# A graph attention layer under a list schedule: allowances on dependences between engines, later small products, and no weight plane on GpSimd

## The chip, the cores and the metric

The kernel runs on one core of a Trainium2 chip. The core has five engines with one instruction queue each: TensorE (PE, with its weight loads as PEld), VectorE (DVE), ScalarE (ACT), GpSimd (POOL) and SyncE (SP, which here only issues DMAs). They run side by side and wait for each other by semaphores. The metric is the time of the launch in microseconds (us); lower is better.

## The reference

One layer of a graph network on 384 nodes with 1024 features. LayerNorm and relu, three projections, a second projection of each, attention of 16 heads of 64 with an additive mask that is built from 6528 edges, an output projection and the residual:

```
h = relu(layernorm(x))                       # 384 x 1024
q, k, v = h @ wq.T + bq, h @ wk.T + bk, h @ wv.T + bv
q2, k2, v2 = (q @ wiq.T + biq), (k @ wik.T + bik), (v @ wiv.T + biv)   # 16 heads of 64
mask = full((384, 384), -inf)
mask[src, dst] = softplus(edge_type_weights)[edge_type - 1]   # the last write of a cell holds
scores = q2 @ k2.T / 8 + mask                # each head
out = softmax(scores) @ v2
return x + out @ wo.T + bo
```

(On the diagonal, a cell that no edge has set gets the fourth weight.) Everything is float32.

## The kernel before, in words

**Products.** Each float32 operand is split in two planes, hi and lo, and a product is three matmuls in a row, hi·hi, hi·lo and lo·hi (`mm3`, L448, L449, L450). The seven 1024 x 1024 weights are read as 56 chunks of 512 KB: v is chunks 0 to 7, q 8 to 15, iv 16 to 23, k 24 to 31, then iq and ik in turns 32 to 47, and o 48 to 55. For each chunk SP loads it (`raw`, or `scan` for a first pass that only sums up norms, L146), ACT makes the hi plane (`split_hi`, L121 or L125) and `split_lo` the lo plane: L132 with a scale, L134 without. L134 runs on DVE, but a list of flags, `lop`, puts it on POOL for chunks 10 and 30 (its flag for 21 has no effect, since only v, q and k chunks are asked). Chunk 1's lo plane is POOL's too, written out in the head.

**Small products.** Scales are taken from bounds, which PE sums over partitions with products of eight or nine columns (L530, L535), or turns around with a transpose. Task names: bv (bound of v), biv, turn (maximum of q), kb, v2t, gq, gk and ob. bv needs the eight v tiles: each is scaled by DVE (`v_f`, L477) and biased and summed by ACT (`v_e`, L480 and L481).

**Mask.** DVE detects for each of 51 columns of 128 edges which of them a later edge overwrites (L293), and forms indices (L299, L300). POOL scatters each column with an indirect DMA into one of three tables in DRAM (L304). When all are done POOL loads the tables (L312, three times `mbs`, 128 x 1152), DVE merges each (L316, three times `ma`), and scales the three row blocks (L567).

**Attention.** For each pair of heads p (0 to 7) and block of 128 rows there is a step S(j), j = 3p to 3p + 2: six matmuls (L702) into the two PSUM banks of tag `s`. DVE adds the mask and reduces (L710, twice), which frees the banks for S(j + 1); ACT takes the exponential (L714), DVE the reciprocal (L717, L721), POOL normalises some of the tiles (L724), ACT makes hi planes (L729, L731) and POOL or DVE the lo planes (L735, L737). SP turns them with DMA transposes (L742), and PE multiplies by v2 (L751, "av"). ACT and DVE split the result (L755, L758), and the o product reads it. DVE finishes seven pieces (L772) with residual x + bo, which POOL has added up before (`residual`, L778, six times), and SP writes them out.

**What sets the order.** After the head, every operation is a task: an engine, an estimated duration, dependences and a lag. PE's order comes from numbers in the table P: chunks follow each other, the small products have a place of their own (`sp`), S(j) is placed at TB + pre + j · rate + ds[j] (TB is the end of chunk 31), av and o relative to it. A loop then picks, again and again, the ready task with the smallest pair (start, due) over all engines, where due is worked back from those who need it, and emits it. So P decides what stands before what in each engine's queue; the queues run in order. The start of a task is the end of what it depends on, plus the lag where that is on another engine; PE's tasks have another allowance, `slack`, on top. `sdl` says how long a scatter takes to land.

Of the kernel before, what the change touches and what calls it, by code (L numbers as in the profile page):

```python
# [23 lines left out]


P = dict(
    pre=11.3,
    rate=2.57,
    avlag=7,
    slack=0.42,  # L30
    act0=6.95,
    dve0=4.68,
    pool0=7.97,
    pb=6,
    lead=3,
    gate=2.88,
    sdl=4.44,
    mll=3.72,
    ds=[0.0, 0.0, 0.0, 0.0, 0.0, 0.0, 0.0, 0.0, 0.0, 0.0, 0.0, 0.62, 0.0, 1.11, 0.0, 0.0, 0.0, 0.0, 0.0, 0.0, 0.0,
        0.0, 0.0, 0.67],  # L40
    da=[1.19, 1.19, 1.19, 1.19, 1.19, 0.13, 0.13, 0.13],
    pool=[0, 1, 0, 1, 0, 1, 0, 1, 0, 1, 0, 1, 0, 1, 0, 1, 0, 1, 0, 1, 0, 1, 0, 1, 0, 0, 0, 1, 0, 1, 0, 1, 0, 1, 0,
        1, 0, 1, 0, 1, 0, 1, 0, 1, 0, 1, 0, 1],
    lop=[0, 0, 0, 0, 0, 0, 0, 0, 0, 0, 1, 0, 0, 0, 0, 0, 0, 0, 0, 0, 0, 1, 0, 0, 0, 0, 0, 0, 0, 0, 1, 0],
    last=[3, 1, 2, 0, 4, 6, 5],
    sp=dict(row=5.6, bv=37.0, biv=53.34, turn=69.41, kb=88.0, v2t=110.0, gq=118.19, gk=128.67, ob=150.0),
    due=dict(v2l=-0.13, ss=-0.34, gkd=-2.65),
)


# [1 line left out]
def gnn_kernel(ctx: ExitStack, tc: tile.TileContext, x, edges, erows, etw, wq, wk, wv, wiq, wik, wiv, wo,  # L52
# [74 lines left out]
    def split_lo(w, eng=None):  # L127
        if w < NCH:
            hi, lo = whl[w]
            sc = weight_scale(w)  # L130
            if sc is not None:
                nc.vector.scalar_tensor_tensor(lo, raw[w], sc, hi, op0=OP.mult, op1=OP.subtract)  # L132
            else:
                (eng or nc.vector).tensor_tensor(lo, raw[w], hi.bitcast(F32), OP.subtract)  # L134
# [520 lines left out]
    bob = scan[:, 2, :]  # L655
# [10 lines left out]
    def task(name, eng, dur, fn, deps=(), lag=0.2, takes="", frees_at=None):  # L666


        tasks[name] = (eng, dur, fn, [d for d in deps if d in tasks or d in end], lag)
        alloc[name] = takes.split()  # L670
        frees[name] = frees_at or []
# [6 lines left out]
    def chunk_mm(c, k):  # L678
        if k == 0:
            gps[c] = bank("g")  # L680
        colmm(gps[c], c, {"iq": qT, "ik": kT.get("t")}.get(chunks[c][0], hT), k)
# [112 lines left out]
    def planes_tasks(c):  # L794
        n = chunks[c][0]
        if c >= 5:
            task(("load", c), "SP", 1.46, lambda: load(c), [("lo", c - 4), ("load", c - 1)], 0.95)
        if c >= 3:
            task(("hi", c), "ACT", 0.95 if n in "vqk" else 1.04, lambda: split_hi(c),
                 [("load", c), ("hi", c - 1), {"iv": "bivd", "iq": "gqd", "ik": "gkd", "o": "obd"}.get(n, "")], 0.2,  # L800
                 "w w" if n in "vqk" else "w", [final(c)] if n != "o" else ["never"])
        if c >= 2:
            pool = c < 32 and n in "vqk" and P["lop"][c]
            task(("lo", c), "POOL" if pool else "DVE", 2.3 if pool else 1.2,
                 lambda: split_lo(c, POOL if pool else None), [("hi", c)])

    def chunk0():
        gps[0] = ps = bank("g")
# [10 lines left out]
    def chunk_tasks(c):  # L819
        n, m = chunks[c]  # L820
        planes_tasks(c)
        before = final(c - 1) if c else ""
        if c == 0:
            task(("mm", 0, 7), "PE", 4.2, chunk0, [("lo", 0)], 0.2, "g", [evict(0)])
        elif n == "iv":
            for i in range(6):
                task(("mm", c, i), "PE", 0.65, lambda i=i: iv_mm(m, i),
                     [("lo", c), ("vlo", m), before] if i == 0 else [("mm", c, i - 1)], 0.2,
                     "ssroag"[i] if m == 0 else "", [("v2l", i) if i < 5 else "early"])
        else:  # L830
            for k in range(KT):
                task(("mm", c, k), "PE", 0.52 if c < 32 else 0.49, lambda k=k: chunk_mm(c, k),
                     [("lo", c), before] if k == 0 else [("mm", c, k - 1)], 0.2, "" if k else "g", [evict(c)])

    def pe_sums(name, bankname, fn, deps, users):
# [126 lines left out]
        task(("aohi", p), "ACT", 0.56, lambda p=p: ao_hi(p), [("av", p), "home"])  # L962
        task(("aolo", p), "DVE", 0.53, lambda p=p: ao_lo(p), [("aohi", p)])
    for i in range(6):
        task(("res", i), "POOL", 1.2, lambda i=i: residual(i), [("xb", i // 2), "bob"])
    OFROM = [[], ["ob"], [("mm", 47, 0)], [("mm", 47, 0), ("o", 2, 0)], [("S", J - 1)], [("S", J - 1), ("o", 4, 0)],
             [("mm", 47, 0), ("o", 3, 0)]]
    for k in range(8):
# [58 lines left out]
    def needed(n):  # L1027
        if n not in due:
            eng, dur, _, _, lag = tasks[n]
            due[n] = 0.0  # L1030
            far = n[0] == "sc"
            d = min([needed(u) - (P["sdl"] + 1 if far and u != ("sc", n[1] + 1) else 0 if tasks[u][0] == eng else lag)
                     for u in users[n]], default=now) - dur
            k = "elo" if n[0] == "lo" and len(n) == 3 else n[0] if isinstance(n, tuple) else n
            due[n] = min(d, at.get(n, d)) + P["due"].get(k, 0.0)
        return due[n]
# [10 lines left out]
    while left:  # L1047
        best = None
        for n, (eng, dur, _, deps, lag) in left.items():
            if not all(d in end for d in deps):  # L1050
                continue
            start = max([free[eng], free["port"] if port(n, eng) else 0.0])
            for d in deps:
                e = tasks.get(d, ("", 0, 0, 0, 0.0))
                start = max(start, end[d] + (0 if e[0] == eng else e[4] + (P["slack"] if eng == "PE" else 0)))
            if eng == "SP" and 0 < dur and n[0] != "turn":
                start = max(start, free["DMA"] - P["gate"])
            ok = True
            for i, tag in enumerate(alloc[n]):
                w = len(ring[tag]) + alloc[n][:i].count(tag) - RING[tag]  # L1060
                for f in ring[tag][w] if w >= 0 else []:
                    if f in end:
                        start = max(start, end[f] + (0 if tasks[f][0] == eng else tasks[f][4]))
                    else:
                        ok = False
            if ok:
                rank = (start, at[n] if eng == "PE" else needed(n))
                if best is None or rank < best[0]:
                    best = rank, n
        if best is None:  # L1070
            raise ValueError(str([(n, [d for d in left[n][3] if d not in end], alloc[n]) for n in list(left)[:12]]))
        (start, _), n = best
        eng, dur, fn, _, lag = left.pop(n)
        end[n] = free[eng] = start + dur
        if port(n, eng):
            free["port"] = end[n]
        if eng == "SP" and 0 < dur and n[0] != "turn":

            free["SP"] = start + 0.48
            end[n] = free["DMA"] = max(free["DMA"], start + 1.1) + dur  # L1080
        if n[0] == "sc":
            end["sd", n[1]] = max(free["DMA"], start + 1.0) + P["sdl"]
        for i, tag in enumerate(alloc[n]):
            ring[tag].append([frees[n][i]] if len(frees[n]) > i else [])
        fn()
# [39 lines left out]
```

## Time and profile before

| | |
|---|---|
| three runs | 280.84, 280.05, 282.71 us; median 280.84 |
| the profiled execution | 280.18 us, of which 278.5 are its span |
| mean granted PE clock | 0.994 |
| busy PE, DVE, ACT, POOL | 267.0, 213.3, 207.1, 141.5 us |
| matmuls | 1629 |

The span runs from the first to the last instruction that the profiler sees; 1.7 us of the time lie outside it. A row of a timeline gives the start in us from the span's start, the duration in us, the engine, the line of the program, the operation, output <- inputs by the program's names, shapes, and in brackets the engine's idle time before it with what ended that. PE's matmuls overlap: the step from one start to the next counts, not the duration. A window's row gives each engine's busy time in a stretch and the granted clock of PE, 1.00 at full speed.

### The profile page before, as it was taken

Reading aid. Unit: us, or ns where it says so; the run is one execution under the profiler, and the core shown is the slowest. Engines: PE = TensorE matmul, PEld = TensorE weight load, DVE = VectorE, ACT = ScalarE, POOL = GpSimd, SP = SyncE. Lnnn points to the kernel's source line nnn. Section 1 sums busy time; section 2 is a strip of 40 time slices with the busy share of each in tenths; the row PEclk is TensorE's granted clock in tenths of the full one; section 3 lists DMA queues with packets and bytes.
Section 4 is the critical chain, followed back from the end, with each engine's and each line's share of the span. In section 5 each row is a group of like instructions: output and inputs, shape, how many; then the busy total and the mean of one; then the engine's idle time right before and its main releaser. Section 6 shows DMA issues by size and latency. Waiting matters only on the chain.

```text
span 278.5 us, 4982 instructions
## 1 busy us (share of the span) xinstructions
PE 267.0 (96%) x1629; PEld 186.7 (67%) x1629; DVE 213.3 (77%) x531; ACT 207.1 (74%) x394; POOL 141.5 (51%) x150
## 2 busy tenths in 40 slices
PE   7999999699999999999999969999999999999995
PEld 5899999599984444899996534545555554444542
DVE  4876679999999634577869597888889997996334
ACT  3898699698989964669859447799889989747300
POOL 4768857465565645105744087556664365505200
PEclk9999999999999999999999997999999999999999
DMA  7799997899999977578688972798989999983706
GB/s 255 258 320 410 402 404 290 335 407 328 345 384 409 401 260 280 175 270 317 236 283 319 373 286 75 125 204 184 210 192 160 225 199 189 243 203 81 141 2 226
DMA packets 59546, 72.44 MB, mean 260 GB/s; under 512 B 42624, under 2 KB 44160, under 8 KB 59520
## 3 DMA queue, kind: packets, MB, share of 16 engines
q1 hardware_dynamic: 57456, 70.32, 80.8%
q0 software_dynamic: 2064, 1.80, 2.2%
q8 instruction: 13, 0.21, 0.3%
q14 instruction: 13, 0.11, 0.1%
HBM read 59.27 MB, written 3.39 MB: 225 GB/s over the span
## 4 chain that ended last, share of the span: by engine, by line
PE 59%; DMA 13%; DVE 11%; ACT 8%; issue 5%; POOL 3%; SPq 1%; DVEq 0%; POOLq 0%; ACTq 0%
PE g L448 13%; PE g L449 13%; PE g L450 13%; DMA scan<-in_wiv_dram 4%; PE s L702 4%; DMA raw<-in_wik_dram 3%; PE a L751 3%; PE s L448 2%; PE s L450 2%; PE s L449 2%; DMA pt<-pp 2%; DMA raw<-in_wo_dram 2%; DVE e L710 2%; DMA g<-in_x_dram 2%; DVE whl L132 2%
## 5 line engine op out<-in xcount | busy, mean ns | idle before, releaser
L448 PE MATMUL g<-g,whl 128*128 128x384 f32 (+1 forms) x312 | 104.7, 336 | 0.0
L449 PE MATMUL g<-g,whl 128*128 128x384 f32 (+1 forms) x312 | 103.8, 333 | 0.0
L450 PE MATMUL g<-g,whl 128*128 128x384 f32 (+1 forms) x312 | 103.8, 333 | 0.0
L304 POOL DMA_INDIRECT tab<-edge x51 | 57.6, 1129 | 39.1 <-DMA tab<-edge 24.1
L146 ACT ACTIVATE scan<-scan 128x1024 f32<-128x1024 f32 x40 | 41.9, 1049 | 8.5 <-DMA scan<-in_wik_dram 4.9
L735 POOL TENSOR_TENSOR pp<-e,pp 128x384 f16<-128x384 f32 x23 | 23.5, 1021 | 29.1 <-ACT pp L729 28.9
L448 PEld LDWEIGHTS g<-g,whl 128*128 128x128 f32 x184 | 34.6, 188 | 2.9 <-DVE whl L134 2.8
L450 PEld LDWEIGHTS g<-g,whl 128*128 128x128 f32 x184 | 34.5, 188 | 0.1
L449 PEld LDWEIGHTS g<-g,whl 128*128 128x128 f32 x184 | 34.6, 188 | 0.0
L714 ACT ACTIVATE e<-e,st 128x384 f32<-128x384 f32 x48 | 29.0, 605 | 7.3 <-DVE st L710 6.7
L134 DVE TENSOR_TENSOR whl<-raw,whl 128x1024 fp32r<-128x1024 f32 x20 | 24.8, 1243 | 11.9 <-ACT whl L125 11.7
L710 DVE CUSTOM_DVE_ANT_0 e<-s,ma,cols 128x384 f32<-128x384 f32 x48 | 27.9, 612 | 4.6 <-PE s L702 3.3
L724 POOL TENSOR_TENSOR e<-e,st 128x384 f32<-128x384 f32 x23 | 23.3, 1015 | 15.9 <-DVE st L721 15.5
L125 ACT ACTIVATE whl<-raw 128x1024 fp32r<-128x1024 f32 x23 | 24.2, 1052 | 2.8 <-DMA raw<-in_wv_dram 2.0
L121 ACT ACTIVATE whl<-raw,cols 128x1024 f16<-128x1024 f32 x16 | 18.0, 1138 | 7.1 <-DMA raw<-in_wiq_dram 3.3
L132 DVE SCALAR_TENSOR_TENSOR whl<-raw,cols,whl 128x1024 f16<-128x1024 f32 x16 | 20.5, 1289 | 2.8 <-ACT whl L121 1.8
L448 PEld LDWEIGHTS <-whl 128*128 128x128 f16 x128 | 12.6, 99 | 14.1 <-issue 7.3
L132 DVE SCALAR_TENSOR_TENSOR whl<-raw,small,whl 128x1024 f16<-128x1024 f32 x16 | 20.2, 1276 | 2.2 <-ACT whl L121 2.2
L121 ACT ACTIVATE whl<-raw,small 128x1024 f16<-128x1024 f32 x16 | 18.1, 1139 | 4.0 <-DMA raw<-in_wo_dram 2.8
L293 DVE SCALAR_TENSOR_TENSOR junk<-rows,edge,upper 128x128 bf16<-128x128 f32 x51 | 18.7, 408 | 0.7 <-DMA rows<-krow 0.7
L702 PE MATMUL s<-k,q 64*128 64x384 f16 x144 | 16.5, 330 | 2.1 <-DVE st L710 2.1
L450 PEld LDWEIGHTS <-whl 128*128 128x128 f16 x128 | 12.7, 99 | 8.6 <-issue 0.5
(206 smaller groups left out, 482.9 us busy)
## 6 DMA issues: line engine op xcount, KB each, us to landing
raw<-in_wv_dram SPq DMA_DIRECT2D x8, 512.0 KB
scan<-in_wiv_dram SPq DMA_DIRECT2D x8, 512.0 KB
raw<-in_wq_dram SPq DMA_DIRECT2D x8, 512.0 KB
scan<-in_wk_dram SPq DMA_DIRECT2D x8, 512.0 KB
raw<-in_wiv_dram SPq DMA_DIRECT2D x8, 512.0 KB
scan<-in_wiq_dram SPq DMA_DIRECT2D x8, 512.0 KB
raw<-in_wk_dram SPq DMA_DIRECT2D x8, 512.0 KB
scan<-in_wik_dram SPq DMA_DIRECT2D x8, 512.0 KB
```

The costliest lines, as they stand in the source:

```text
L121: nc.scalar.activation(hi, raw[w], AF.Copy, scale=sc)
L125: nc.scalar.activation(hi, raw[w], AF.Copy)
L132: nc.vector.scalar_tensor_tensor(lo, raw[w], sc, hi, op0=OP.mult, op1=OP.subtract)
L134: (eng or nc.vector).tensor_tensor(lo, raw[w], hi.bitcast(F32), OP.subtract)
L146: ACT.activation(x, x, AF.Abs if n in ("iv", "o") else AF.Square, accum_out=l1[:, j, m:m + 1])
L304: nc.gpsimd.indirect_dma_start(out=tabs[c // RNG], out_offset=bass.IndirectOffsetOnAxis(ap=idx[:, c:c + 1], axis=0), in_=val[:, c:c + 1], ...
L448: nc.tensor.matmul(ps, lhi, rhi, start=first, stop=False)
L449: nc.tensor.matmul(ps, lhi, rlo, start=False, stop=False)
L450: nc.tensor.matmul(ps, llo, rhi, start=False, stop=last)
L702: nc.tensor.matmul(sps[j][o][:, :N], q[r, a, t * 128:(t + 1) * 128], k[r, b, :], start=(i == 0), stop=(i == 2))
L710: DVE.tensor_tensor_reduce(es[j][o], sps[j][o][:, :N], ma[:, j % 3, :], nscale, 3.0e38, OP.add, OP.min, sts[j][:, o:o + 1])
L714: ACT.activation(es[j][o], es[j][o], AF.Exp, bias=sts[j][:, o:o + 1], scale=-1.0, accum_out=sts[j][:, 2 + o:3 + o])
```

## The change

It edits the table P and the rules of the planner; no operation computes anything else.

- PE's order: pre, rate and ds move the S steps; `sp` moves bv, biv, turn, v2t and gk.
- `lop` goes: the lo planes of chunks 10 and 30 are made by DVE.
- The planner's allowances on dependences between engines: `slack` for PE is 0.64 where it was 0.42; a new `wait`, 0.09, for the other engines; a new `late`, 0.3, for whatever waits for a task of SP (a load). The due times of lo planes move by 1.37.
- The selects (`sel`) are planned not before TB + 4.5 + 1.54 i. Scatters are planned to land 5.6 after their start, whatever DMA has queued (`sdl` is gone).
- A residual add depends on the softmax lo plane (20, 1).
- Some estimated durations of matmul groups are 0.01 lower.

```diff
 P = dict(
-    pre=11.3,
-    rate=2.57,
+    pre=12.85,
+    rate=2.66,
     avlag=7,
-    slack=0.42,
-    act0=6.95,
+    slack=0.64,
+    act0=6.77,
...
-    gate=2.88,
-    sdl=4.44,
+    gate=2.96,
...
-    ds=[0.0, 0.0, 0.0, 0.0, 0.0, 0.0, 0.0, 0.0, 0.0, 0.0, 0.0, 0.62, 0.0, 1.11, 0.0, 0.0, 0.0, 0.0, 0.0, 0.0, 0.0,
-        0.0, 0.0, 0.67],
+    ds=[0.0, 0.0, 0.0, 0.0, 0.0, 0.0, 0.0, 0.47, 0.47, 0.47, 0.47, 1.09, 0.47, 1.58, 0.47, 0.47, 0.47, 0.47, 0.62,
+        0.47, 0.47, 0.47, 0.47, 1.14],
...
-    lop=[0, 0, 0, 0, 0, 0, 0, 0, 0, 0, 1, 0, 0, 0, 0, 0, 0, 0, 0, 0, 0, 1, 0, 0, 0, 0, 0, 0, 0, 0, 1, 0],
     last=[3, 1, 2, 0, 4, 6, 5],
-    sp=dict(row=5.6, bv=37.0, biv=53.34, turn=69.41, kb=88.0, v2t=110.0, gq=118.19, gk=128.67, ob=150.0),
-    due=dict(v2l=-0.13, ss=-0.34, gkd=-2.65),
+    sp=dict(row=5.6, bv=41.0, biv=55.0, turn=71.05, kb=88.0, v2t=111.14, gq=118.19, gk=126.78, ob=150.0),
+    due=dict(v2l=-0.13, ss=-0.34, gkd=-2.65, lo=1.37),
+    wait=0.09,
+    late=0.3,
+    selat=4.5,
+    selby=1.54,
 )
...
         if c >= 2:
-            pool = c < 32 and n in "vqk" and P["lop"][c]
-            task(("lo", c), "POOL" if pool else "DVE", 2.3 if pool else 1.2,
-                 lambda: split_lo(c, POOL if pool else None), [("hi", c)])
+            task(("lo", c), "DVE", 1.2, lambda: split_lo(c), [("hi", c)])
...
-        task(("res", i), "POOL", 1.2, lambda i=i: residual(i), [("xb", i // 2), "bob"])
+        task(("res", i), "POOL", 1.2, lambda i=i: residual(i), [("xb", i // 2), "bob", ("lo", 20, 1)])
...
-                start = max(start, end[d] + (0 if e[0] == eng else e[4] + (P["slack"] if eng == "PE" else 0)))
+                start = max(start, end[d] + (0 if e[0] == eng else e[4] + (P["slack"] if eng == "PE" else P["late"] if e[0] == "SP" else P["wait"])))
             if eng == "SP" and 0 < dur and n[0] != "turn":
                 start = max(start, free["DMA"] - P["gate"])
+            if n[0] == "sel":
+                start = max(start, TB + P["selat"] + n[1] * P["selby"])
...
         if n[0] == "sc":
-            end["sd", n[1]] = max(free["DMA"], start + 1.0) + P["sdl"]
+            end["sd", n[1]] = start + 5.6
```

The changed file has two lines more in P, so most lines have a number two higher than before (L477 becomes L479).

How the order of instructions changes, at three places. DVE around the last two v tiles, before (L134 is a lo plane, L477 a v tile, L293 a detection, L299 and L300 the indices):

```order
L134 TENSOR_TENSOR whl<-raw,whl 128x1024
L477 TENSOR_TENSOR f<-g,rrow 128x384
L293 SCALAR_TENSOR_TENSOR junk,edge<-rows,edge,upper 128x128 x7
L299 SCALAR_TENSOR_TENSOR ed<-edge 128x3x3
L300 TENSOR_SCALAR edge<-ed,small 128x3x3
L293 SCALAR_TENSOR_TENSOR junk,edge<-rows,edge,upper 128x128
L477 TENSOR_TENSOR f<-g,rrow 128x384
L134 TENSOR_TENSOR whl<-raw,whl 128x1024
```

and the same place now:

```order
L479 TENSOR_TENSOR f<-g,rrow 128x384
L136 TENSOR_TENSOR whl<-raw,whl 128x1024
L295 SCALAR_TENSOR_TENSOR junk,edge<-rows,edge,upper 128x128 x8
L136 TENSOR_TENSOR whl<-raw,whl 128x1024
L479 TENSOR_TENSOR f<-g,rrow 128x384
L301 SCALAR_TENSOR_TENSOR ed<-edge 128x3x3
L302 TENSOR_SCALAR edge<-ed,small 128x3x3
L295 SCALAR_TENSOR_TENSOR junk,edge<-rows,edge,upper 128x128 x2
```

The last v tile has one weight plane more ahead of it on DVE. On PE the product that waits for it, bv, stands at row 231 of the order where it stood at 204; each matmul of that place is one row, its weight load being part of it.

POOL behind the last scatters, before (L312 loads the tables, L778 is the residual add, L724 and L735 belong to the softmax):

```order
L304 DMA tab_104<-edge 147584x1
L312 DMA mbs<-tab_102 128x3x384
L312 DMA mbs<-tab_103 128x3x384
L312 DMA mbs<-tab_104 128x3x384
L778 TENSOR_TENSOR g_1720<-g_1720,scan 128x512 x4
L724 TENSOR_TENSOR e<-e,st 128x384
L778 TENSOR_TENSOR g_1720<-g_1720,scan 128x512 x2
L735 TENSOR_TENSOR pp<-e,pp 128x384
```

and now the end of POOL's queue:

```order
L737 TENSOR_TENSOR pp<-e,pp 128x384
L726 TENSOR_TENSOR e<-e,st 128x384
L780 TENSOR_TENSOR g_1724<-g_1724,scan 128x512
L737 TENSOR_TENSOR pp<-e,pp 128x384
L726 TENSOR_TENSOR e<-e,st 128x384 x2
L737 TENSOR_TENSOR pp<-e,pp 128x384 x2
L780 TENSOR_TENSOR g_1724<-g_1724,scan 128x512 x5
```

The six residual adds have gone from behind the table loads to the end. The two L134 of POOL (one between the scatters of chunk 10's time, one with ten scatters behind it) are gone from its queue.

DVE from the k bound's last step (L564) to the first mask scaling, before (L316 merges a table, L132 is a lo plane, L572 and L580 a k tile and its lo plane, L693 a lo plane of q2 or k2):

```order
L564 TENSOR_SCALAR cols<-cols 128x1
L572 TENSOR_TENSOR f<-g,rrk 128x384
L132 SCALAR_TENSOR_TENSOR whl<-raw,cols,whl 128x1024 x2
L580 SCALAR_TENSOR_TENSOR g_1414<-f,cols,g_1414 128x384
L132 SCALAR_TENSOR_TENSOR whl<-raw,cols,whl 128x1024
L693 SCALAR_TENSOR_TENSOR q_1763<-g,cols,q_1763 128x384
L132 SCALAR_TENSOR_TENSOR whl<-raw,cols,whl 128x1024
L693 SCALAR_TENSOR_TENSOR k_1800<-g,cols,k_1800 128x384
L316 COPY_PREDICATED ma<-mbs 128x1152
L132 SCALAR_TENSOR_TENSOR whl<-raw,cols,whl 128x1024
L316 COPY_PREDICATED ma<-mbs 128x1152
```

and now:

```order
L566 TENSOR_SCALAR cols<-cols 128x1
L318 COPY_PREDICATED ma<-mbs 128x1152
L134 SCALAR_TENSOR_TENSOR whl<-raw,cols,whl 128x1024
L574 TENSOR_TENSOR f<-g,rrk 128x384
L134 SCALAR_TENSOR_TENSOR whl<-raw,cols,whl 128x1024 x2
L582 SCALAR_TENSOR_TENSOR g_1429<-f,cols,g_1429 128x384
L695 SCALAR_TENSOR_TENSOR q_1771<-g,cols,q_1771 128x384
L134 SCALAR_TENSOR_TENSOR whl<-raw,cols,whl 128x1024
L318 COPY_PREDICATED ma<-mbs 128x1152
L695 SCALAR_TENSOR_TENSOR k_1802<-g,cols,k_1802 128x384
L318 COPY_PREDICATED ma<-mbs 128x1152
L569 TENSOR_SCALAR ma<-ma,cols 128x384 x2
```

The first merge now stands right behind the k bound, ahead of the weight planes, and two of the three scalings stand ahead of one more weight plane, one q2 lo plane and the third, behind which comes the first L712 (L710 before).

More of the change, by code (lines that the diff above doesn't have):

```diff
@@ L826, in chunk_tasks @@
             for i in range(6):
-                task(("mm", c, i), "PE", 0.65, lambda i=i: iv_mm(m, i),
+                task(("mm", c, i), "PE", 0.64, lambda i=i: iv_mm(m, i),
                      [("lo", c), ("vlo", m), before] if i == 0 else [("mm", c, i - 1)], 0.2,
@@ L831, in chunk_tasks @@
             for k in range(KT):
-                task(("mm", c, k), "PE", 0.52 if c < 32 else 0.49, lambda k=k: chunk_mm(c, k),
+                task(("mm", c, k), "PE", 0.511 if c < 32 else 0.481, lambda k=k: chunk_mm(c, k),
                      [("lo", c), before] if k == 0 else [("mm", c, k - 1)], 0.2, "" if k else "g", [evict(c)])
@@ L1031, in needed @@
             far = n[0] == "sc"
-            d = min([needed(u) - (P["sdl"] + 1 if far and u != ("sc", n[1] + 1) else 0 if tasks[u][0] == eng else lag)
+            d = min([needed(u) - (4.6 if far and u != ("sc", n[1] + 1) else 0 if tasks[u][0] == eng else lag)
                      for u in users[n]], default=now) - dur
```

## The prediction

> **What bounds the kernel now.** I read the busy times of the page first, then the waits of TensorE, then the timeline around the two waits that are large, then the windows around them for the clock.
>
> The first lines of the page, the waits of TensorE (engine, line, releaser: us in total, times, longest), and three windows (us, then busy time and count of PE, PEld, DVE, ACT, POOL, the granted PE clock, DMA share, GB/s):
>
> ```profile
> span 278.5 us, 4982 instructions
> PE 267.0 (96%) x1629; PEld 186.7 (67%) x1629; DVE 213.3 (77%) x531; ACT 207.1 (74%) x394; POOL 141.5 (51%) x150
> ...
> PE s L530 <- ACT f L481: 2.7, 1, 2.7
> PE s L702 <- DVE st L710: 2.1, 2, 1.9
> ...
> PE o L449 <- DVE whl L132: 0.4, 1, 0.4
> PE s L448 <- DVE st L710: 0.2, 1, 0.2
> ...
> 60.00:150.00 90.00, 90.00 (x489) 70.97 (x489) 67.50 (x167) 71.50 (x114) 45.63 (x40) 1.00 0.85 309
> 150.00:164.30 14.30, 14.30 (x91) 8.24 (x89) 10.84 (x12) 7.42 (x12) 3.65 (x3) 1.00 1.02 385
> 164.30:166.90 2.60, 0.52 (x3) 0.18 (x2) 2.45 (x6) 1.84 (x3) 2.60 (x3) 1.00 0.25 99
> 166.90:170.40 3.50, 3.46 (x14) 1.41 (x14) 3.02 (x6) 3.38 (x7) 3.18 (x3) 0.53 0.06 9
> ```
>
> PE is busy 267.0 of 278.5 us, and 90.00 of 90 between 60 and 150: its matmuls are the bound, and the change leaves their number alone. Only what stands between them can go. That is two waits (2.7 and 2.1), two crumbs (0.4 and 0.2), and behind the second wait 3.5 us at a clock of 0.53.
>
> The first wait, by the timeline (start, us, engine, line, operation, tiles, [idle before <- releaser]), PE, DVE, ACT and POOL in turn:
>
> ```profile
> 48.70 0.33 PE L450 MATMUL g<-g,whl 128*128 128x384 f32 x1
> 49.22 0.34 PE L450 MATMUL g<-g,whl 128*128 128x384 f32 x1
> 52.24 0.17 PE L530 MATMUL s<-l,small 128*128 128x8 bf16 x1 [2.68 <-ACT f L481]
> ...
> 45.47 2.78 DVE L293 SCALAR_TENSOR_TENSOR junk<-rows,edge,upper 128x128 bf16<-128x128 f32 x1
> 48.51 0.34 DVE L293 SCALAR_TENSOR_TENSOR junk<-rows,edge,upper 128x128 bf16<-128x128 f32 x1
> 50.34 0.55 DVE L477 TENSOR_TENSOR f<-g,rrow 128x384 f32<-128x384 f32 x1
> ...
> 51.57 0.52 ACT L481 ACTIVATE f<-g 128x384 f32<-128x384 f32 x1
> ...
> 45.67 2.43 POOL L134 TENSOR_TENSOR whl<-raw,whl 128x1024 fp32r<-128x1024 f32 x1
> ```
>
> The bound sum of v (L530) needs the last v tile: L477 on DVE, then L480 and L481 on ACT. DVE is late because one small edge detection took 2.78 us instead of 0.34, exactly beside the lo plane that POOL makes (2.43). So 2.44 us of the 2.68 were lost there.
>
> The second wait is the first attention masks' chain. POOL's queue, then DVE's, then PE's:
>
> ```profile
> 127.70 2.40 POOL L134 TENSOR_TENSOR whl<-raw,whl 128x1024 fp32r<-128x1024 f32 x1 [15.18 <-ACT whl L125]
> 146.64 0.96 POOL L304 DMA_INDIRECT tab<-edge  x1 [2.28 <-DMA scan<-in_wo_dram]
> 151.82 0.75 POOL L312 DMA_DIRECT2D mbs<-tab  x1 [2.16 <-DMA tab<-edge]
> 161.40 6.52 POOL L778 TENSOR_TENSOR g<-g,scan 128x512 f32<-128x512 f32 x4 [8.84 <-DMA scan<-in_bo_dram]
> ...
> 146.66 0.15 DVE L564 TENSOR_SCALAR cols<-cols 128x1 f32<-128x1 f32 x1
> 160.26 1.51 DVE L316 COPY_PREDICATED ma<-mbs 128x1152 f32<-128x1152 int32 x1
> 162.15 2.12 DVE L316 COPY_PREDICATED ma<-mbs 128x1152 f32<-128x1152 int32 x1
> 164.30 1.27 DVE L567 TENSOR_SCALAR ma<-ma,cols 128x384 f32<-128x384 f32 x1
> 165.72 0.62 DVE L710 CUSTOM_DVE_ANT_0 e<-s,ma,cols 128x384 f32<-128x384 f32 x1 [0.15 <-DVE ma L567]
> 173.95 0.41 DVE L567 TENSOR_SCALAR ma<-ma,cols 128x384 f32<-128x384 f32 x1
> ...
> 158.38 0.66 PE L702 MATMUL s<-k,q 64*128 64x384 f16 x6
> 164.18 0.33 PE L450 MATMUL g<-g,whl 128*128 128x384 f16 x1
> 166.40 0.32 PE L702 MATMUL s<-k,q 64*128 64x384 f16 x1 [1.90 <-DVE st L710]
> 167.84 0.50 PE L448 MATMUL g<-g,whl 128*128 128x384 f16 x1
> 170.62 0.33 PE L448 MATMUL g<-g,whl 128*128 128x384 f16 x1
> ```
>
> POOL stood 15.18 us in front of the lo plane of chunk 30, with ten scatters still queued behind it, so the last mask load goes out at 151.82. The third select ends at 164.27, and the last ones are slowed beside the residual adds (2.12 against 1.51; the scaling 1.27 against 0.41). The first softmax reduction (L710) runs at 165.72, and S1, whose banks it frees, waits from 164.35. Then the clock falls.
>
> **What the second wait is worth.** Undisturbed, S1 would start at 164.18 + 0.17 and the next product 0.59 later, as behind S0 (its first matmul at 158.38, the product behind it 0.59 later): 164.94. It starts at 167.84: 2.90 lost. From there to 170.62 stand nine matmuls; at the 0.1625 spacing of full clock they take 1.46, here 2.78: 1.32 lost. Together 4.2 us.
>
> **The change, part by part.** *Lo planes 10 and 30 leave POOL.* These groups (busy us, mean ns, idle before) give the prices:
>
> ```profile
> L134 DVE TENSOR_TENSOR whl<-raw,whl 128x1024 fp32r<-128x1024 f32 x20 | 24.8, 1243 | 11.9 <-ACT whl L125 11.7
> L132 DVE SCALAR_TENSOR_TENSOR whl<-raw,cols,whl 128x1024 f16<-128x1024 f32 x16 | 20.5, 1289 | 2.8 <-ACT whl L121 1.8
> L304 POOL DMA_INDIRECT tab<-edge x51 | 57.6, 1129 | 39.1 <-DMA tab<-edge 24.1
> ```
>
> DVE gets 2 x 1.24. For plane 30 it has cover: between 60 and 150 it is idle 90 − 67.5 = 22.5 us. For plane 10 it pays 1.24 and is spared 2.44.
>
> *The bound sum moves back.* In PE's order it stands at row 231 where it stood at 204: 27 matmuls of 0.173 (three steps from 48.70 to 49.22 take 0.52), so it is due at 49.56 + 4.7 = 54.2. The v tile: 52.1 − 2.44 + 1.24 = 50.9, and with one lo plane more ahead of it in the new DVE order 52.1. Margin 2 us or more; if DVE is held up again by more than that, the excess returns. I take **−2.7**; bounds −2.7 and 0. The other moved sums (biv, turn, kb, v2t) show no wait before and stand later, or gk at the same place: nothing.
>
> *The mask chain moves forward.* The ten scatters go on at 112.5 (127.70 − 15.18). One costs (57.6 + 39.1 − 15.2) / 51 = 1.6 us, or 1.9 with that idle time in, which I take: 131.5. The last mask load was issued 5.2 us after the last scatter's start, so now near 137, and its landing is bounded by the third select, 10.3 us on: 147 at most; the first is issued ahead of that. DVE's order has the first select straight behind the gk block, which ended at 146.81 and now, 2.7 earlier, at 144.1. From there to the first L710 stand 3 selects (1.51), 5 lo planes (1.29), 3 scalings (0.41), 3 qlo, one k tile and its lo (0.6 each, an estimate from the 0.62 of L710): 4.5 + 6.45 + 1.2 + 3.0 = 15.2. So L710 runs from 159.3, and its pair is through at about 160.4. For S1: in PE's order S0 begins at row 1026 where it began at 1008 (two rows a matmul there, its weights and itself, so 9 matmuls later), and S1 at 1074 instead of 1086 (33 products between the two before, 18 now), so S1 is due (15 − 9) x 0.1625 = 1.0 earlier, at 164.35 − 2.7 − 1.0 = 160.7. Its bank comes free about when it is due: a wait of 0 to 1, say 0.5. A gap so short I take to leave the clock alone, since the 2.68 at 49.6 was followed by no slower spacing. So **−4.2 + 0.5**. If chunk loads are late again, DVE's 15.2 stretches; but the 1.8 MB of mask tables (3 x 128 x 1152 x 4 bytes) no longer fall into 150 to 164, where DMA is at 1.02 and 385 GB/s: 4.6 us of traffic less there.
>
> *The residual adds* leave the mask chain's side and run at the end, five of them behind POOL's last lo plane:
>
> ```profile
> 260.77 0.91 POOL L735 TENSOR_TENSOR pp<-e,pp 128x384 f16<-128x384 f32 x1 [0.63 <-ACT pp L729]
> 270.52 0.75 DVE L772 SCALAR_TENSOR_TENSOR g<-g,small,g 128x512 f32<-128x512 f32 x1 [2.11 <-PE g L450]
> ```
>
> At 6.52 / 4 = 1.63 each they take 8.2 from 261.7, so to 269.9, while the first finish starts at 270.52: covered, barely for the fifth, which only a later finish needs. The one placed earlier holds up one POOL lo plane by 1.6; its transposes and the product that reads them come S steps later. Nothing; bounds 0 and +1.6.
>
> *Attention is paced anew.* The o products come in from S14 on and S22 stands next to S23, with only three matmuls (0.65) between. S23 then waits for the reductions of S22: 2 x 0.54 + 0.15, less 0.65, is 0.6; with a lo plane ahead on DVE 1.9. I take **+0.9**. Elsewhere:
>
> ```profile
> 191.43 0.66 PE L702 MATMUL s<-k,q 64*128 64x384 f16 x6
> 219.90 0.50 PE L702 MATMUL s<-k,q 64*128 64x384 f16 x4
> ```
>
> Nine S in 28.5 us is 3.16 each, without a wait of PE. The new order's tightest stretch, S1 to S7, has 34 triples of matmuls (0.4875) and six S (0.59), 20.1 us: 3.35 each. Tight for DVE, so +0.4, bounds 0 and +4.6 (below). The 0.4 and 0.2 go: their products have moved away from the late planes: −0.6.
>
> **The sum**: −2.7 − 4.2 + 0.5 + 0.9 + 0.4 − 0.6 = −5.7, of a span of 278.5: 272.8. The profiled execution took 280.18, 1.7 more than its span: 274.5. The median, 280.84, lies 0.66 above the profiled one; adding half of that, **274.8**. With every stall gone (−7.5) it is 272.7, the floor.
>
> **Rivals.** *The clock stretch is not the gap's* (0.06). After 2.05 us of idle PE it fell; after 2.68 at 49.6 it did not. If length doesn't decide, the 1.3 lost behind S1 and some of the slow S1 may fall elsewhere: 276.3. [...]
>
> *DVE can't keep the pace* (0.15). Before, S1 to S7 took 191.43 − 166.40 = 25.0 us, with the late masks in it. If DVE, not PE, set that, the 20.1 us of the new order stretch by up to 4.9 and the gain of the second wait is given back: 278 to 280, no change. Against it: 3.16 held later with as many softmax operations; for it: two weight planes per S pair fall into this stretch. It decides once DVE needs over 3.4 us per S.
>
> *Slower: the select blocks DVE* (0.07). The first select now stands ahead of the weight planes of the first (iq, ik) chunks. DVE runs in order, so if the first table lands after about 145, every us is one of PE's. With scatters as slow as DMA made some (24.1 us of waits on their own landing, all perhaps in the busy stretch) and the loads as late as before, 155, PE loses up to 10: 274.8 + 10 = 285. It is slower than before from a landing past 151.
>
> *The tail* (0.07): the five adds and the finishes hold each other up, as the adds and the selects did (2.12 for 1.51, so 40% more): 8.2 becomes 11.4, to 273.1 for the last add, with finishes from 270.52 on waiting 2 to 3: 277 to 278.
>
> **Chances.** Forecast 0.65, the rest as above. A measurement of this kernel tells about 1% from no change, that is 278.0 and 283.6. Faster: 0.65 + 0.06 + a third of 0.15 + most of 0.07 = 0.80, trimmed to 0.79; same 0.14; slower 0.07. The range runs from the floor, 272.5, to 279.3, which takes in the tail and most of DVE's pace and leaves out the blocked select.
>
> **What would show it.** Right: no wait of L530 on ACT; POOL's last scatter near 131; first L710 near 159; no stretch of clock below 0.9 after 60; PE's waits in all under 3 us behind the head. Wrong: waits of L702 on L710 summing to over 4; PE waiting for L132 at 145 to 150 behind a select; finishes released by POOL.

## The result, and the profile after

| | before | after |
|---|---|---|
| median of the runs | 282.04 us (279.49 to 285.37, 12 runs) | 277.89 us (275.11 to 279.82, 12 runs) |
| the profiled execution | 280.18 us | 277.94 us |
| its span | 278.5 us | 276.0 us |
| PE busy in it | 267.0 us | 266.0 us |

The ratio is 0.985, with a 95% interval of 0.980 to 0.990: a gain of 1.5 per cent. Medians are of all runs of a kernel, while a ratio sets against each other only those that lie within 1.5 per cent of their kernel's fastest, so it need not be the quotient of the medians. The change was timed a second time, on another occasion, at 0.992 (0.987 to 0.997). Forecast was 274.8 and a range of 272.5 to 279.3. So the time lies in the range, 3.1 us above the forecast, and the sign is right. Forecast was a gain of 2.2 per cent (274.8 against 280.84); measured is two thirds of that, and little over a third by the second timing. With more runs the median of before rose by 1.2 us.

The first lines of the page of after, and the waits of TensorE:

```profile
span 276.0 us, 4965 instructions
PE 266.0 (96%) x1629; PEld 185.6 (67%) x1629; DVE 214.6 (78%) x533; ACT 207.9 (75%) x394; POOL 133.3 (48%) x148
...
PE g L452 <- DVE whl L134: 1.5, 1, 1.5
PE g L392 <- POOL ident masks.py:199: 1.4, 1, 1.4
PE s L372 <- ACT g L360: 0.9, 1, 0.9
PE g L450 <- DVE f L479: 0.8, 1, 0.8
PE g L372 <- DVE g L364: 0.8, 1, 0.8
PE a L753 <- DVE g L760: 0.6, 1, 0.6
PE g L507 <- DVE cols L498: 0.3, 1, 0.3
PE s L704 <- DVE st L712: 0.2, 1, 0.2
```

Both large waits of before are gone (nothing on L532, which was L530, and 0.2 on the S steps), and so are its two crumbs. In their place stand four that before did not have: 1.5, 0.8, 0.6 and 0.3. The waits of the head (L392 and L372) sum to 3.1 where they were 2.7. Idle PE time was 278.5 − 267.0 = 11.5 and is 10.0; the other 1.0 us is less busy time. No stretch at half clock is left while PE works: the granted clock is 1.00 up to 274.5, and PE's last matmul starts at 272.2.

The mask chain of after, POOL first, then DVE, then PE with the product that waits for the weight plane and the first two S steps (start, us, engine, line, operation, tiles, idle before and its end):

```profile
115.72 0.96 POOL L306 DMA_INDIRECT tab<-edge  x1 [0.30 <-issue]
...
130.60 1.14 POOL L306 DMA_INDIRECT tab<-edge  x1 [0.61 <-DMA tab<-edge]
133.34 1.63 POOL L314 DMA_DIRECT2D mbs<-tab  x2 [1.60 <-DMA tab<-edge]
135.22 0.75 POOL L314 DMA_DIRECT2D mbs<-tab  x1 [0.25 <-DMA tab<-edge]
...
148.54 0.15 DVE L566 TENSOR_SCALAR cols<-cols 128x1 f32<-128x1 f32 x1
148.62 1.53 DVE L318 COPY_PREDICATED ma<-mbs 128x1152 f32<-128x1152 int32 x1
150.03 1.28 DVE L134 SCALAR_TENSOR_TENSOR whl<-raw,cols,whl 128x1024 f16<-128x1024 f32 x1
...
162.53 0.61 DVE L712 CUSTOM_DVE_ANT_0 e<-s,ma,cols 128x384 f32<-128x384 f32 x1
...
151.37 0.34 PE L452 MATMUL g<-g,whl 128*128 128x384 f16 x1 [1.47 <-DVE whl L134]
160.53 0.66 PE L704 MATMUL s<-k,q 64*128 64x384 f16 x6
164.16 0.66 PE L704 MATMUL s<-k,q 64*128 64x384 f16 x6
```

The row at 115.72 is the first of the ten scatters that stood behind plane 30. The last scatter starts at 130.6 and the last table load at 135.2, 16.6 us sooner than before. But the k bound ends at 148.7, and the select and the weight plane stand behind it; PE waits 1.47 for that plane at 151.37. Why the bound is late, ACT's queue shows. The rows are k's sixth and seventh hi planes (L579) and norm sums of o's chunks (L148):

```profile
138.78 0.62 ACT L579 ACTIVATE g<-f,cols 128x384 f16<-128x384 f32 x1 [0.48 <-DVE f L574]
141.36 1.06 ACT L148 ACTIVATE scan<-scan 128x1024 f32<-128x1024 f32 x1 [1.95 <-DMA scan<-in_wo_dram]
144.23 1.06 ACT L148 ACTIVATE scan<-scan 128x1024 f32<-128x1024 f32 x1 [1.72 <-DMA scan<-in_wo_dram]
145.28 0.60 ACT L579 ACTIVATE g<-f,cols 128x384 f16<-128x384 f32 x1
```

The hi plane at 145.28 has nothing to wait for by itself; its tile was ready at 141.9 (DVE's row of L574 starts at 141.34 and takes 0.56). It stands behind two sums that wait for loads, and DVE's lo plane, the k bound and the select stand behind it.

### The profile page after: what moved, and what is told of

It reads as the page before. It is cut to its first block, busy times and chain, and to the rows that moved or that the text cites. A ratio compares the mean times of both kernels' runs of the same rounds, so it can differ in the third digit from the quotient of the medians.

```text
span 276.0 us, 4965 instructions
## 1 busy us (share of the span) xinstructions
PE 266.0 (96%) x1629; PEld 185.6 (67%) x1629; DVE 214.6 (78%) x533; ACT 207.9 (75%) x394; POOL 133.3 (48%) x148
## 4 chain that ended last, share of the span: by engine, by line
PE 57%; DMA 17%; ACT 12%; DVE 5%; issue 4%; SPq 2%; POOL 1%; ACTq 0%; DVEq 0%
PE g L450 12%; PE g L452 11%; PE g L451 11%; DMA raw<-in_wq_dram 7%; PE s L704 5%; PE a L753 5%; DMA scan<-in_wiv_dram 4%; ACT scan L148 3%; DMA scan<-in_wo_dram 3%; ACT whl L127 2%; DMA raw<-in_wiv_dram 2%; PE s L450 2%; PE s L452 2%; PE s L451 2%; ACT vhl L639 1%
## 5 line engine op out<-in xcount | busy, mean ns | idle before, releaser
L148 ACT ACTIVATE scan<-scan 128x1024 f32<-128x1024 f32 x40 | 42.0, 1050 | 9.4 <-DMA scan<-in_wo_dram 3.7
L726 POOL TENSOR_TENSOR e<-e,st 128x384 f32<-128x384 f32 x23 | 21.4, 929 | 43.1 <-DVE st L723 40.1
L136 DVE TENSOR_TENSOR whl<-raw,whl 128x1024 fp32r<-128x1024 f32 x22 | 27.1, 1230 | 14.1 <-ACT whl L127 6.5
L127 ACT ACTIVATE whl<-raw 128x1024 fp32r<-128x1024 f32 x23 | 24.2, 1052 | 8.8 <-DMA raw<-in_wv_dram 3.3
L712 DVE CUSTOM_DVE_ANT_0 e<-s,ma,cols 128x384 f32<-128x384 f32 x48 | 27.7, 611 | 2.2 <-PE s L704 1.7
L134 DVE SCALAR_TENSOR_TENSOR whl<-raw,small,whl 128x1024 f16<-128x1024 f32 x16 | 20.5, 1295 | 3.1 <-ACT whl L123 3.1
L134 DVE SCALAR_TENSOR_TENSOR whl<-raw,cols,whl 128x1024 f16<-128x1024 f32 x16 | 20.4, 1279 | 0.0
L450 PEld LDWEIGHTS <-g 128*128 128x128 f16 x104 | 10.2, 98 | 12.5 <-issue 3.0
L739 DVE SCALAR_TENSOR_TENSOR pp<-e,st,pp 128x384 f16<-128x384 f32 x25 | 17.3, 699 | 1.5 <-ACT pp L733 1.3
```

Of the source, the lines that this page charges most:

```text
L127: nc.scalar.activation(hi, raw[w], AF.Copy)
L148: ACT.activation(x, x, AF.Abs if n in ("iv", "o") else AF.Square, accum_out=l1[:, j, m:m + 1])
L450: nc.tensor.matmul(ps, lhi, rhi, start=first, stop=False)
L712: DVE.tensor_tensor_reduce(es[j][o], sps[j][o][:, :N], ma[:, j % 3, :], nscale, 3.0e38, OP.add, OP.min, sts[j][:, o:o + 1])
```

## The experiments

In all but the last two the planner is left alone: the plan of before or of after is made as it is, then single tasks are moved in the finished order, with everything else at its place. `move(a, b, True)` puts task a behind task b, without True ahead of it.

```diff
-        fn()
+        seq.append((n, fn))
+
+    def move(n, to, behind=False):
+        i = [m for m, _ in seq].index(n)
+        t = seq.pop(i)
+        j = [m for m, _ in seq].index(to)
+        seq.insert(j + behind, t)
+
+    ...                          # the moves of the experiment
+    for n, fn in seq:
+        fn()
```

Ratios are to the kernel before, timed on the same chip in the same series.

### Which part of the change gains

**The two planes alone.**

```diff
-                 lambda: split_lo(c, POOL if pool else None), [("hi", c)])
+                 lambda: split_lo(c), [("hi", c)])
```

> The order of before, with the lo planes of chunks 10 and 30 made by DVE at the place where POOL made them; nothing else moves. Theory 1 (the two planes on POOL are the root of both waits): the detection beside plane 10 takes 0.34 instead of 2.78, so PE's wait at L530 falls from 2.68 to 0.2 to 0.5; the ten scatters no longer stand behind plane 30, the mask loads go out before 140 instead of at 151.8, chunk loads after 150 come sooner, and S1's wait of 2.1 and the slow clock behind it shrink to under 1 in all. Time 5 to 6 us below before. Theory 2 (each part of the change cures its own wait; DVE's order and the residual adds beside it are what delays the first reduction): L530's wait falls likewise, S1's stays at 1.5 to 2 with the clock stretch. Time 2.2 to 2.7 us below before.

Measured: 278.5 us, ratio 0.988 (0.984 to 0.992), profiled span 275.2. Its waits, and the place where L530 stood waiting before:

```profile
PE s L702 <- DVE st L710: 1.1, 2, 0.8
...
51.20 0.34 PE L450 MATMUL g<-g,whl 128*128 128x384 f32 x1
51.38 0.18 PE L530 MATMUL s<-l,small 128*128 128x8 bf16 x1
51.42 0.42 PE L448 MATMUL g<-g,whl 128*128 128x384 f32 x1
```

L530 follows at once, at its old place in the order. But PE came there 2.0 us later than in before (51.20 against 49.22 for the product ahead of it), because its head had taken longer. The v tile's last step on ACT ended at 50.15, 0.6 behind 49.56, when L530 was due in before. In the kernel with planes and adds, below, PE came in time and L530 waited 0.6. So the planes alone take some 2 us of the 2.7. S1 waits 1.1 instead of 2.1, and no half clock follows (the mean granted clock of this execution is 1.000). That is between the two theories in size (3.9 us of median), and it is most of what the whole change brings. The first theory holds for most of the first wait and half of the second.

**The bound sum of v alone.**

```diff
+    move("bv", ("mm", 9, 5), True)
+    for a, b in (("bvd", "bv"), (("vhi", 0), "bvd"), (("vlo", 0), ("vhi", 0))):
+        move(a, b, True)
```

> The order of before with the bound sum of v placed 18 matmuls later on PE (3.1 us), and the four tasks behind it that read it moved along; planes 10 and 30 stay on POOL. All theories: the wait of L530 (2.68) goes, and S1's wait stays, since POOL's queue, the mask chain and the residual adds are as before; 2.5 to 2.7 us below before. [...]

Measured: 281.56 us (278.61 to 285.31), ratio 0.996 (0.990 to 1.001): no change that can be told. In its profiled execution, of 283.70 us, L530 still waits 1.18, though it stands 3.1 later: the v tile came 1.8 later than in before's (52.18 against 50.34). And a new wait of 2.8 stands at the turn of q's maximum (L505), where what was won ahead of it is lost again, in this one execution. S1's wait stayed, 2.0, as expected. The clock stayed at 1.00 behind it (168.84 to 172.26), where it fell in before, and was at 0.50 behind the wait at the turn instead (86.93 to 90.34).

**The residual adds alone.**

```diff
+    for i in range(6):
+        move(("res", i), ("res", i - 1) if i else ("lo", 23, 1), True)
```

> The order of before with the six residual adds moved behind POOL's last lo plane. Theory 2 (the adds slow the last select, 2.12 for 1.51, and the scaling, 1.27 for 0.41): the first reduction comes 1.5 us earlier and S1 waits 0.5 to 0.7 instead of 2.1; with so short a gap no slow clock, 1.5 to 3.5 us below before. Theory 1 (late tables and late chunk loads set the place of the selects): the same 1.5 us, since the selects and the scaling lie between the tables and S1 in either case, but not more, and L530's wait stays 2.7. A loss of 1 us or more would show that adds at the end delay the finishes.

Measured: 280.44 us, ratio 0.996 (0.991 to 1.000). Without the adds beside them the last select took 1.49 and the scaling 0.42, together 1.5 us less than in before, so the size forecast for the contention holds in their durations. S1's wait fell from 2.1 to 0.24, but that is not the adds' doing alone: PE came to S1 3.5 us later than in before (the product ahead of it at 167.69 against 164.18), and the last select had waited 1.25 for its table. The gain of 2 us of median is at the edge of what can be told; in its profiled execution L530 waited 3.6 instead of 2.7, though nothing ahead of it differs from before, and the mean granted clock was 0.988 where before's was 0.994. That wait varied by about 1 us between these two executions.

**Both of these together, planes and adds.** The two edits above, no new order and no allowances.

> The order of before with planes 10 and 30 on DVE and the six residual adds behind POOL's last lo plane: two parts of the change, and none of its new order or allowances. With the planes alone S1 still waited 1.1, behind a select of 2.11 and a scaling of 1.27 beside the adds. Theory 2 for that rest: 0.6 + 0.9 are saved on DVE and S1's wait goes, 1 us below the planes alone, so a span near 274 and a time as good as after or better, 1.5 to 2 per cent below before. If S1 then waits for something else (the loads), the same as with the planes alone.

Measured: 276.37 us (275.16 to 277.06, 4 runs), ratio 0.983 (0.975 to 0.991). The selects run at 1.5 and the scaling at 0.42, and PE waits for no S step:

```profile
160.47 1.53 DVE L316 COPY_PREDICATED ma<-mbs 128x1152 f32<-128x1152 int32 x1
162.04 0.42 DVE L567 TENSOR_SCALAR ma<-ma,cols 128x384 f32<-128x384 f32 x1
162.62 0.62 DVE L710 CUSTOM_DVE_ANT_0 e<-s,ma,cols 128x384 f32<-128x384 f32 x1 [0.15 <-DVE ma L567]
```

Two of the change's parts, in the old order, are as good as the whole, as far as four runs can tell. The profiled span, 275.4, was not the 274 expected: waits of 0.9 (o's plane), 0.9 (the last av), 0.6 (L530) and some of 0.3 to 0.5 remain.

### What the new order costs

**Plane 30 back on POOL, in the new order.**

```diff
+    seq[[n for n, _ in seq].index(("lo", 30))] = ("lo", 30), lambda: split_lo(30, POOL)
+    for i in range(41, EC):
+        move(("sc", i), ("sc", i - 1) if i > 41 else ("lo", 30), True)
```

> The order of after, but plane 30 on POOL again and the last ten scatters behind it, as before had them. The first select stands right behind the k bound on DVE here, ahead of the weight planes. The rival 'the select blocks DVE': the tables are loaded from about 149 on instead of 133, the first select starts at 153 or later instead of 148.6, and PE's wait for the weight plane at 151 grows from 1.5 to 5 to 7: 4 to 6 us above after, so at or above before. If tables are not what the select waits for (DVE has other work to do in that time), under 2 us above after.

Measured: 285.29 us (281.00 to 287.04), ratio 1.004 (0.997 to 1.011), where after had 0.985 in its series: slower than after, and not to be told from before. The profiled execution is the slowest of the ten, 287.04. DVE and PE of it:

```profile
155.61 1.44 DVE L318 COPY_PREDICATED ma<-mbs 128x1152 f32<-128x1152 int32 x1 [9.03 <-DMA mbs<-tab]
156.94 1.27 DVE L134 SCALAR_TENSOR_TENSOR whl<-raw,cols,whl 128x1024 f16<-128x1024 f32 x1
...
158.27 0.50 PE L452 MATMUL g<-g,whl 128*128 128x384 f16 x1 [7.65 <-DVE whl L134]
```

DVE stands 9 us in front of the select, which waits for its table, with the weight plane behind it, and PE waits 7.65, where 5 to 7 was expected. By the two ratios the kernel is 1.9 per cent above after, some 5 us, within the 4 to 6 expected. The rival of the prediction is a real mechanism, and the freed POOL queue keeps the changed kernel off it.

**k's seventh hi plane ahead of the two norm sums.** Only ACT's order changes:

```diff
+    move(("ss", 35), ("ke", 6), True)
+    move(("ss", 36), ("ss", 35), True)
```

> The order of after, with one edit on ACT: the hi plane of k's seventh tile stands ahead of the two norm sums of o's chunks 3 and 4, which wait for their loads. Theory 3 (the wait of 1.5 at 151 in after comes from ACT's queue: a short task that the k bound waits for stands behind two that wait for DMA): the k bound ends 3 to 4 us sooner (near 145 instead of 148.7), the first select with it, and PE's wait for the weight plane goes, 1.2 to 1.7 us below after. Rival (the select ahead of the weight planes is the cause, or the tables land late): the select starts sooner at most by 1 us, and the wait stays over 1.

Measured: 275.68 us (274.69 to 277.43, 4 runs), ratio 0.983 (0.974 to 0.992), span 273.5. ACT and DVE of it:

```profile
140.91 0.62 ACT L579 ACTIVATE g<-f,cols 128x384 f16<-128x384 f32 x1 [2.61 <-DVE f L574]
141.44 1.04 ACT L148 ACTIVATE scan<-scan 128x1024 f32<-128x1024 f32 x1
...
144.53 0.15 DVE L566 TENSOR_SCALAR cols<-cols 128x1 f32<-128x1 f32 x1
160.02 0.61 DVE L712 CUSTOM_DVE_ANT_0 e<-s,ma,cols 128x384 f32<-128x384 f32 x1
```

The k bound ends at 144.7 instead of 148.7, the wait for the weight plane is 0.04, and the first reduction comes at 160.0. Theory 3 stands for the wait: it came from ACT's queue. A gain in time over after is not shown, since the interval takes in after's 0.985.

**The same for the row factor in the head.**

```diff
+    move("rowc", ("hi", 4))
+    move(("vf", 0), ("lo", 3))
```

> The order of after, with two tasks moved in the head of the schedule: the row factor of LayerNorm (ACT) ahead of the hi plane of chunk 4, and the first v tile (DVE) ahead of the lo plane of chunk 3. Theory 3 (the wait of 0.8 at 25.5 is the same thing again: the row factor stands behind a plane that waits 1.6 for its load): the wait goes, 0.6 to 1.0 us below after. Rival (PE waits there for chunk 4's own load in any case): the wait moves to a weight plane, no gain.

Measured: 277.82 us, ratio 0.988 (0.985 to 0.992): no gain. The wait at 25.5 went as expected. The one at 151 was 0.12, though ACT's order there is that of after: one of the two norm sums had its load in time, and the hi plane stood 2.0 behind its tile instead of 3.4. So the price of that place, too, hangs on when loads land. But the turn of q's maximum now waited 1.87: the head start was lost at the next place where DVE is late.

**Both, and two edits on PE.**

```diff
+    move("turn", ("mm", 17, 3), True)
+    move(("av", 6), ("o", 4, 5), True)
```

> The order of after with the edits of the two kernels above, and two on PE: the turn of q's maximum one product group later (0.65), and the seventh av ahead of two o products instead of behind them, so that the eighth does not wait for its bank. If PE's waits add up: 0.8 + 1.5 + 0.3 + 0.6 = 3.2 us below after, a span near 273. If a wait that is taken away comes back at the next place (S1, whose bank came free 1 us early), 1.5 to 2.5.

Measured: 276.15 us (274.79 to 277.86, 4 runs), ratio 0.984 (0.975 to 0.994), span 273.7. Of PE's waits behind the head 1.1 is left (turn 0.45, the last av 0.43, S23 0.22). In the profiled execution 2.3 us of the span went, which is within the second expectation, 1.5 to 2.5. In time this kernel can't be told from after either.

**After and the k plane once more, side by side.**

> The changed kernel once more, as the measure for the kernel beside it: 0.98 to 0.99 of before, with PE's waits at 25 and 151 in its profile.

> The changed kernel with k's seventh hi plane ahead of two norm sums on ACT once more, beside after on the same chip. Theory 3: 1 to 2 us below after, 0.978 to 0.984 of before. If what it gained the first time was the state of that chip, the same as after.

Measured: after 279.0 us, ratio 0.992 (0.987 to 0.997), a little above what was expected; the k plane first 279.0 us (4 runs), ratio 0.987 (0.966 to 1.007). The order between them is not shown by this. The two profiles show that the wait at 151 is not all that decides. In after the wait of 1.49 at 150 came back; with the k plane first there is none there in this run either. But the row factor's place (L355, behind chunk 4's hi plane L127) gave 0 in the one and 2.6 in the other. ACT of after, then ACT and PE of the k plane first:

```profile
21.34 1.06 ACT L127 ACTIVATE whl<-raw 128x1024 fp32r<-128x1024 f32 x1 [0.53 <-DMA raw<-in_wv_dram]
22.31 0.48 ACT L355 ACTIVATE rrow<-s 128x384 f32<-128x384 f32 x1
```

```profile
24.45 1.06 ACT L127 ACTIVATE whl<-raw 128x1024 fp32r<-128x1024 f32 x1 [3.70 <-DMA raw<-in_wv_dram]
25.41 0.47 ACT L355 ACTIVATE rrow<-s 128x384 f32<-128x384 f32 x1
...
27.41 0.41 PE L450 MATMUL g<-g,whl 128*128 128x384 f32 x1 [2.63 <-DVE f L479]
```

The two programs do not differ here. Chunk 4's load came 3.1 us later in one execution, and the row factor, the first v tile and PE's next bank stood behind it; PE's wait there was 0 and 2.6 in these two, 0.8 in the profile of after above, and 0.25 in the first run of the k plane first. In before the row factor stands ahead of that plane. So the new order has a place whose price is set by when one load lands. Whether that makes the spread of after's runs, 275.1 to 279.8, is not shown; before, which does not have this place, spreads as far (279.5 to 285.4).

### The allowances

**After without them** (slack 0.42, wait 0, late 0; the planner plans anew).

```diff
-    slack=0.64,
+    slack=0.42,
...
-    wait=0.09,
-    late=0.3,
+    wait=0.0,
+    late=0.0,
```

> The changed kernel with the planner's allowances as before (slack 0.42, wait 0, late 0); the new places of the small products, the S steps, the selects, planes on DVE and residual adds stay. Theory 1 (the gain is the planes', and the allowances only reshuffle queues): the same time as after within 1 per cent, with other small waits; the wait at 25.5 goes, since the row factor stands ahead of chunk 4's plane again. Theory 4 (the allowances make room between engines, so that S and small products don't wait): PE's waits behind the head grow from 3.4 to 6 or more, 2 us or more above after.

Measured: 280.37 us, ratio 0.993 (0.986 to 0.999); the same as after, which had 0.992 in this series, within the intervals. The row factor is ahead again and its wait is gone; 1.2 at the turn and many of 0.1 to 0.4 are there instead. Theory 4 finds no support, though a gain of half a per cent from the allowances is not excluded.

**Before with them alone.**

```diff
-    slack=0.42,
+    slack=0.64,
...
-                start = max(start, end[d] + (0 if e[0] == eng else e[4] + (P["slack"] if eng == "PE" else 0)))
+                start = max(start, end[d] + (0 if e[0] == eng else e[4] + (P["slack"] if eng == "PE" else 0.3 if e[0] == "SP" else 0.09)))
```

> The kernel before with the three allowances alone (0.64 for PE, 0.3 behind loads, 0.09 for the rest); planes 10 and 30 stay on POOL, small products and residual adds as the plan of before puts them. Theory 1: POOL's queue still stands in front of plane 30 with scatters behind it, and detection beside plane 10 is still held up; within 1 per cent of before. Theory 4: 1 per cent or more below before.

Measured: 296.09 us (291.64 to 298.43, 4 runs) against 282.39 for before: 4 to 5 per cent slower, and a miss for both theories. The first reduction, at 172.88, stands behind planes that wait for late chunk loads (DVE waited 3.92 for a hi plane of ACT, which had waited 4.06 for its load), and the S steps wait 8.3 in all. So these allowances are no good by themselves in the old plan; places and allowances were chosen together, and a plan with one of them changed is another program.

## Why the prediction was right, and where its sum was off

**The bound.** Right: PE is busy 266 of 276 us, and only what stands between matmuls has changed.

**The wait at L530: −2.7.** The size is right, the step in part. I took the whole of it with the bound sum's later place. The planes alone take some 2 us of it at the old place and leave 0.6; the later place alone removes half of it, and in the profiled execution the gain is lost again at the next small product. The v tile's end was put at 50.9, and at 52.1 with one plane more ahead of it; it came at 50.9 with that plane ahead: in after, L483 runs from 50.36 for 0.53.

**The second wait and the slow clock: −4.2 + 0.5.** Both are gone, as forecast. The last scatter (131.5 forecast, 130.6 measured) and the last load (137, 135.2) came near where they were put, the scatter with some luck: the ten began at 115.7 instead of 112.5 and took 1.65 each instead of 1.9, and the two errors cancel. The step that failed is "the gk block at 144.1". I took its end from before and moved it by the first wait alone, and did not ask what stands ahead of the tasks it needs in ACT's queue. It ended at 148.7, and the first reduction came at 162.5, not 159.3. S1 did not wait only because PE was late itself: it came to S1 at 164.2, where 160.7 had been worked out. Nor did all of this term come back: 2.1 of its 4.2 was busy time of PE (4.2 less the waits of 1.90 and 0.22), and PE's busy time fell by 1.0.

**The terms that were missing.** The sum had no wait for the weight plane (1.47), the first v tile (0.79), the last av's bank (0.57) and the turn (0.32): 3.15 us. Two of them arise on ACT, where a short task stands in the queue behind one that itself waits for a load; the new order shows that, and the trace of before cannot. The av's could have been read off: one o product stands between the last two av in the new order, and there is one bank for both. Against them S23 waited 0.22 where +0.9 was taken, and the tightened S steps nothing where +0.4 was: 0.5 + 0.9 + 0.4 − 0.22 = 1.6 to the good. 272.8 + 3.15 − 1.6 = 274.4; the span was 276.0, and of the 1.6 left over 0.4 is in the waits of the head (3.1 for 2.7); the rest is in steps that I can't name one by one. That the time stayed in the range is in part luck: 1.6 had been set aside for waits that did not come.

**The residual adds: nothing.** Right, with room to spare. Five took 6.16 us, where 8.2 was taken, and ended at 264.4; the first finish starts at 268.06:

```profile
258.26 6.16 POOL L780 TENSOR_TENSOR g<-g,scan 128x512 f32<-128x512 f32 x5
...
268.06 0.75 DVE L774 SCALAR_TENSOR_TENSOR g<-g,small,g 128x512 f32<-128x512 f32 x1 [2.18 <-PE g L452]
```

And they do what was said beside the selects: with the planes moved and the adds left, select and scaling took 2.11 and 1.27; with both moved they took 1.53 and 0.42.

**The rivals.** One sign of the blocked select came, PE waiting 1.47 for a weight plane behind it, but not its cause. The tables were loaded in time, and the select ran as soon as the k bound was through; with the hi plane moved on ACT the wait went, though the select still stood ahead of the planes. With plane 30 on POOL the rival itself came, at 7.65. Of the other signs, the first reduction (162.5 for 159) and PE's waits behind the head (3.4 for under 3) missed. DVE's pace and the tail did not show. The clock's rival was put wrongly, as the last section shows: the slow stretches there stand behind gaps, but of two gaps of 2.68 and 2.66 one had such a stretch behind it and one had not, so it was not length alone.

## What to carry to other kernels

When instructions are moved in an engine's queue, look at each short task that many wait for, and at what stands right ahead of it: here one that waited for a DMA handed its lateness on to all of them, and with it the scatter from run to run (a load 3.1 us later, and PE's wait 2.63 instead of 0). Of a change of many parts, try the one that takes work off a blocked queue alone; here two parts of it in the old order did as well as the whole plan, as far as four runs can tell. And a plan's allowances can't be judged without the places that were chosen with them.

## What the runs showed of the hardware

**Gaps of like length had different prices.** In before, a gap of 2.68 at 49.6 cost no clock and one of 2.05 at 164.4 did. Elsewhere it was the other way round: 2.66 at 49.6 did cost it in the kernel with the allowances alone, and 2.0 in front of S1 did not in the one with the bound sum moved. The windows below are 3.41 us long, as long as the slow stretch of before, which runs from 167.12 to 170.53. In each pair but the first, the clock is 1.00 in the first window and 0.50 in the second (us, PE busy and count, PEld, DVE, ACT, POOL, clock, DMA share, GB/s). First before:

```profile
47.65:51.07 3.42, 1.90 (x11) 1.68 (x11) 3.35 (x18) 1.07 (x2) 2.65 (x4) 1.00 0.57 181
51.07:54.48 3.41, 2.24 (x14) 2.24 (x14) 3.31 (x17) 3.35 (x8) 0.71 (x1) 1.00 1.02 408
163.71:167.12 3.41, 1.29 (x9) 0.59 (x9) 3.22 (x7) 2.57 (x6) 3.41 (x3) 1.00 0.36 145
167.12:170.53 3.41, 3.41 (x14) 1.41 (x11) 2.92 (x6) 3.16 (x5) 3.09 (x3) 0.50 0.08 14
```

then the kernel with the allowances alone, and the second run of the k plane first:

```profile
49.23:52.65 3.42, 0.76 (x6) 0.54 (x5) 3.42 (x13) 1.67 (x4) 2.96 (x3) 1.00 1.03 397
52.65:56.06 3.41, 3.41 (x13) 3.41 (x12) 3.24 (x17) 3.41 (x7) 1.64 (x3) 0.50 1.01 410
```

```profile
25.25:28.67 3.42, 1.26 (x7) 1.29 (x8) 3.13 (x9) 2.77 (x12) 0.47 (x2) 1.00 1.04 415
28.67:32.08 3.41, 3.41 (x13) 3.41 (x12) 1.59 (x4) 3.35 (x8) 2.39 (x2) 0.50 1.03 396
```

In the first pair the bound between the windows cuts the gap in two; PE is busy 1.90 and 2.24 in the halves, and the clock is 1.00 in both and on to 163.71. In the other three PE is busy 1.29, 0.76 and 1.26 of the first window, and the second runs at 0.50. What decided in these runs whether the clock fell, how long PE was busy, the number of its matmuls or something else, is not shown.

In these kernels a gap of 2 to 3 us cost either itself, or itself and a slow stretch (1.32 in nine matmuls behind S1 in before).
